# Split weight pieces on GpSimd's DMA queue, and fp8 tokens scaled by ScalarE

## The chip, the cores and the metric

The kernel runs on one core of a Trainium2 chip. The metric is the device time of one execution, in microseconds. The core has five engines that each follow their own list of instructions in order: TensorE (matrix products and transposes), VectorE, ScalarE, GpSimd, and SyncE (SP), which here only issues DMAs. ScalarE and GpSimd can issue DMAs too. In the profile they are called PE, DVE, ACT, POOL and SP; PEld is TensorE's loading of weights. Engines wait for each other through semaphores, and a waiting instruction holds up all that stands behind it on its engine.

## The reference

Two layers of a gated cross-attention block over x, 4 x 512 tokens of 512 features. The first adds an int8 cross-attention to the context and a mixture of experts; the second an fp8 attention with 16 query heads on 8 key heads, and a ternary feed-forward layer. Cut to what matters here:

```python
# layer 0, the experts: 8 experts, 2 per token, plus a shared one
order = jnp.argsort(flat_sel, stable=True)
routed_in = xf[order // TOPK] * top_scores_sorted[:, None]
h = silu(ragged_dot(routed_in, w1, counts)) * ragged_dot(routed_in, w3, counts)
routed_out = ragged_dot(h, w2, counts)

# layer 1, the fp8 attention
def _div_clamp_fp8(x, scale):
    y = jnp.clip(x / scale, -448., 448.)
    return fp8_roundtrip(y.astype(bfloat16))
ln_out = _ln(x, ln_w, ln_b)
q  = _ln(linear(_div_clamp_fp8(ln_out, q_in_scale), wq) * wq_scale, qln_w, qln_b)
k, v, qx  = (the same with scales of their own)
core, xout = softmax(q k / sqrt(128)) v, the same for qx with the context's keys
out = linear(_div_clamp_fp8(concat(core, xout), proj_smooth), wproj) * scales
```

So the tokens are normalized, given an affine, and then divided by four different input scales (q, qx, k, v), each followed by a clip, a rounding to bf16 and one to fp8. The scales are vectors over the features, not scalars.

## The kernel before, in words

The work runs in four stages on the time axis of the profile: the int8 cross-attention (to about 510 us); the routing and the shared expert (to about 703 us); the expert slots and after them the context's keys and values (to about 1360 us); and the fp8 attention with the ternary feed-forward woven in (to the end).

**Split weights.** The fp8 attention's matrix products run in a two-part format: a weight is kept as a high part and a remainder, both fp32r. `split_weights` (L1493 on) cuts the weights in 80 pieces of 128 x 512. A piece (class `Split`) has four steps: `load` brings 256 KB to the tile s_raw (L1519); `centre` multiplies by the input scale (L1525) and, for the query and key heads, takes out the mean over each head (`centred`, L1488 to L1490), on VectorE; `cut` lets ScalarE round to the high part (L1531) and GpSimd subtract it from the whole (L1532), both into s_hl; `store` writes 512 KB to DRAM (L1535). s_raw and s_hl have two buffers each. Of the pieces, 23 are done during the shared expert, step by step in a written order (those carry L245, the line of the helper that records an ordered instruction). The other 57, 33 with centring and 24 of the projection without, are done in the slots, through `__call__`.

**Slots.** Tokens sorted by expert fill 39 slots of 128 rows (loop at L1290). For each slot s, TensorE transposes the rows (`turn_in`), multiplies by w1 and w3 (`up`), transposes the hidden row (`turn_hidden`) and multiplies by w2 (`down`); ScalarE applies silu (L1243), VectorE the gate's product (L1244), and ScalarE scales the result (L1262) and stores it. The weights of an expert come in with `load` (L1193 to L1200, two DMAs of 896 KB) and `load_down` (L1222), on SP's queue, only where the expert differs from that of the slot two before; `load` of slot s + 3 overwrites the buffer of slot s + 1. Rows are loaded and stored on ScalarE's queue. Each pass of the loop also takes one or two split pieces and one step of the ternary weights (t_raw: loads at L2276, sums, scales and codes at L2283 to L2308, stores at L2309; all DMAs on SP). In this stage only TensorE's order is written by hand; a scheduler (Tile) orders the instructions of each other engine by its own estimate of when they can run, and the order that it chooses is fixed in the program.

**Attention.** 32 units (batch, head pair, source) of 16 ticks each. A `Beat` holds for each tick a list of steps by place; the places in order are begin, gate, weighed, divide, evacuate, normal, turned, squares, gated, scores, weigh, project, turn_in, turn, rest, codes, load. All engines are ordered by hand here, so the place fixes the position in each engine's list. The exponentials on ScalarE (g_p) are in "scores". `tokens` (L1930 on) prepares the next batch's tokens while the present one is attended to, for b = 1, 2, 3: load (g_xn), normalize, transpose on TensorE to PSUM (`turn`, place turn_in), `affine` on VectorE to g_ln (place normal), and 16 `code` steps (place codes). A code step calls `scaled` (L1629, VectorE: times the input scale, then the minimum with 448, to a bf16 tile f_y of two buffers) and `coded` (L1618, VectorE: the maximum with -448, the exponent mask f_e, the constant f_c; then two additions on GpSimd, f_t and the result g_xq). The attention's outputs and the feed-forward's rows go through `scaled` and `coded` too.

Evacuations of transposed probabilities (g_pT) go to VectorE or ScalarE, by how much else is entered for the tick; `affine` enters one step for VectorE in that count (the last argument of `at`).

Of the kernel before, what the change touches and what calls it, by code (L numbers as in the profile page):

```python
# [12 lines left out]
BF = mybir.dt.bfloat16  # L13
# [4 lines left out]
AF = mybir.ActivationFunctionType  # L18
ALU = mybir.AluOpType
# [3 lines left out]
P = 128  # L23
B, S, D = 4, 512, 512
# [3 lines left out]
KC = D // P  # L28
# [9 lines left out]
FP8_MAX = 448.0  # L38
# [136 lines left out]
class Router:  # L175
# [46 lines left out]
    def partial(self, PE, pg, b):  # L222

        for c in range(KC):
            PE.matmul(
                pg[ts(c, 32)], lhsT=self.gw[:, c, :], rhs=self.xT[b][:, c, :],
                start=True, stop=True,
            )
# [19 lines left out]
class Beat:  # L248
# [10 lines left out]
    def at(self, tick, place, step, busy=None):  # L259

        if busy is not None:
            self.loads[tick, busy] = self.loads.get((tick, busy), 0) + 1
        self.steps.setdefault(tick, {}).setdefault(self.PLACES.index(place), []).append(step)
# [1220 lines left out]
def centred(k, w, heads, VE):  # L1484

    wv = w.rearrange("p (h d) -> p h d", d=D1)
    m = k.small.tile([P, heads], F32, tag="s_mean")
    VE.tensor_reduce(m, wv, AX.X, ALU.add)  # L1488
    VE.tensor_scalar(m, m, -1.0 / D1, None, ALU.mult)
    VE.tensor_tensor(wv, wv, m[:, :, None].to_broadcast([P, heads, D1]), ALU.add)  # L1490


def split_weights(k):  # L1493

    nc, tc, a = k.nc, k.tc, k.a  # L1500
    s = {
        "q": tc.dram_tile([NP, P, KC, 2, 512], F32, name="s_q"),
        "qx": tc.dram_tile([NP, P, KC, 2, 512], F32, name="s_qx"),
        "kv": tc.dram_tile([NP, P, KC, 2, 512], F32, name="s_kv"),
        "kx": tc.dram_tile([B, NP, TB, P, 2, 2, D1], F32, name="s_kx"),
        "proj": tc.dram_tile([NP, 2, HP, P, 2, 512], F32, name="s_proj"),
    }

    class Split:

        def __init__(self, of, to, scales=(), c=0, heads=0):
            self.of, self.to, self.scales, self.c, self.heads = of, to, scales, c, heads

        def load(self, pool, SY):
            self.pool = pool
            self.raw = pool.tile([P, 512], F32, tag="s_raw", name="s_raw")
            SY.dma_start(self.raw, self.of)  # L1519

        def centre(self, VE):
            n = len(self.scales)
            for i, name in enumerate(self.scales):
                part = self.raw[:, ts(i, 512 // n)]
                VE.tensor_scalar(part, part, k.col(name)[:, self.c : self.c + 1], None, ALU.mult)  # L1525
            if self.heads:
                centred(k, self.raw[:, 0 : self.heads * D1], self.heads, VE)

        def cut(self, AE, GE):
            self.hl = hl = self.pool.tile([P, 2, 512], F32R, tag="s_hl", name="s_hl")  # L1530
            AE.copy(hl[:, 0, :], self.raw)  # L1531
            GE.tensor_tensor(hl[:, 1, :], self.raw, hl[:, 0, :].bitcast(F32), ALU.subtract)  # L1532

        def store(self, SY):
            SY.dma_start(self.to, self.hl.bitcast(F32))  # L1535

        def __call__(self, pool):
            self.load(pool, nc.sync)
            self.centre(nc.vector)
            self.cut(nc.scalar, nc.gpsimd)  # L1540
            self.store(nc.sync)

    steps = []
    for i in range(NP):
        for name in ("q", "qx"):
            steps += [
                Split(a[f"w_{name}"][i, :, c, :], s[name][i, :, c], (f"{name}_in",), c, HP)
                for c in range(KC)
            ]
        steps += [  # L1550
            Split(a["w_kv"][i, :, c, :], s["kv"][i, :, c], ("k_in", "v_in"), c, 2)
            for c in range(KC)
        ]
        steps += [
            Split(a["w_proj"][i, src, h], s["proj"][i, src, h])
            for src in range(2) for h in range(HP)
        ]
    return s, steps


def attend_and_feed(k, scratch, codes8, sources, ffn):
# [13 lines left out]
    nc, tc, a = k.nc, k.tc, k.a  # L1575
    VE, AE, GE, PE = (Ordered(tc, e) for e in (nc.vector, nc.scalar, nc.gpsimd, nc.tensor))
    UNIT = HP * TB
    with ExitStack() as ctx:
        p1 = ctx.enter_context(tc.tile_pool(name="g_1", bufs=1))
        p2 = ctx.enter_context(tc.tile_pool(name="g_2", bufs=2))  # L1580
# [10 lines left out]
        scale = 1.0 / math.sqrt(D1)  # L1591
        rin = codes8.rin
# [23 lines left out]
        at = beat.at  # L1616

        def coded(y, out, n=S):  # L1618

            VE.tensor_scalar(y, y, -FP8_MAX, None, ALU.max)  # L1620
            e = p2.tile([P, S], U16, tag="f_e", name="f_e")[:, 0:n]
            c = p2.tile([P, S], BF, tag="f_c", name="f_c")[:, 0:n]
            VE.tensor_scalar(e, y.bitcast(U16), 0x7F80, None, ALU.bitwise_and)
            VE.tensor_scalar(c, e.bitcast(BF), 2.0**-6, 1.5 * 2.0**20, ALU.max, ALU.mult)
            t = p2.tile([P, S], F32, tag="g_ct", name="f_t")[:, 0:n]
            GE.tensor_tensor(t, y, c, ALU.add)
            GE.tensor_tensor(out, t, c, ALU.subtract)

        def scaled(src, j, n=S):  # L1629
            y = p2.tile([P, S], BF, tag="f_y", name="f_y")[:, 0:n]  # L1630
            VE.tensor_scalar(y, src, rin[:, j : j + 1], FP8_MAX, ALU.mult, ALU.min)
            return y

        def load_w(of, got, key, parts):
# [293 lines left out]
        def tokens(u0, b):  # L1928


            xq, got = [None] * 4, {}

            def stats(src):
                st = sm4.tile([P, 6], F32, tag="ln_st")
                mv = sm4.tile([P, 2], F32, tag="g_mv")
                VE.bn_stats(st, src)
                VE.bn_aggr(mv, st)
                ve = sm4.tile([P, 1], F32, tag="g_ve")
                VE.tensor_scalar(ve, mv[:, 1:2], EPS, None, ALU.add)
                rstd = sm4.tile([P, 1], F32, tag="g_lnr")  # L1940
                GE.tensor_tensor(rstd, ve, k.neghalf[:, :1], ALU.pow)
                return mv, rstd

            def norm(t, part):
                xn = got["xn"][:, t, :]
                if part:
                    mv, rstd = got["st", t]
                    VE.tensor_scalar(xn, xn, mv[:, 0:1], rstd, ALU.subtract, ALU.mult)
                if part < 2:
                    got["st", t] = stats(xn)  # L1950

            def turn(c):
                got["pt"] = pt = ps_p.tile([P, S], F32, tag="ps_p", name="ps_p")
                for t in range(TB):
                    PE.transpose(pt[:, ts(t, P)], got["xn"][:, t, ts(c, P)], k.ident)

            def affine(c):
                got["ln"] = lnT = p1.tile([P, S], F32, tag="g_ln", name="g_ln")
                VE.tensor_scalar(
                    lnT, got["pt"], k.col("ln_w")[:, c : c + 1], k.col("ln_b")[:, c : c + 1],  # L1960
                    ALU.mult, ALU.add,
                )

            def code(c, i):
                if c == 0:
                    xq[i] = codes8.place(i, F32R, f"g_xq{i}_{b}")
                coded(scaled(got["ln"], i * KC + c), xq[i][:, c, :])

            def fetch():
                got["xn"] = xn = p1.tile([P, TB, D], F32, tag="g_xn", name=f"g_xn{b}")  # L1970
                nc.sync.dma_start(xn, ffn.mid[ts(b, TB)].rearrange("t p d -> p t d"))

            at(u0, "load", fetch)
            for t in range(TB):
                for part in range(3):
                    at(u0 + 3 * t + 2 + part, "codes", partial(norm, t, part))
            for c in range(KC):
                m = u0 + UNIT + 1 + 4 * c
                at(m, "turn_in", partial(turn, c))
                at(m + 1, "normal", partial(affine, c), VE)  # L1980
                for n, i in enumerate((0, 2, 3)):
                    at(m + 1 + n, "codes", partial(code, c, i))
                m = u0 + 2 * UNIT + 11 + c
                at(m, "turn_in", partial(turn, c))
                at(m + 1, "normal", partial(affine, c), VE)
                at(m + 1, "codes", partial(code, c, 1))
            return xq

# [208 lines left out]
        xq = sources  # L2197
        for n, (b, i, src) in enumerate(units):
# [4 lines left out]
            if n + 1 < len(units):  # L2203
                nb, ni, nsrc = units[n + 1]
                if nb != b:
                    xq = following
# [213 lines left out]
```

## Time and profile before

| | |
|---|---|
| median of 3 runs | 3403.62 us (3402.86 to 3405.48) |
| the profiled execution, its time | 3405.26 us |
| its span | 3403.6 us |
| mean clock granted to TensorE | 0.983 |
| slots, L1262 of slot 0 to the end | 731 to about 1148 us |
| distance of undisturbed slots | 10.32 us |
| token stretches, first to last affine | 1753.4 to 1871, 2248 to 2367, 2744 to 2862 us |

The profile has the time from the first to the last instruction as its span. A line of the groups reads: source line, engine, operation, output tile <- input tiles with their shapes, the count; busy time in us and the mean of one in ns; the engine's idle time just before them and what ended it. A line of the windows gives the busy time of PE, PEld, DVE, ACT and POOL with instruction counts, then the granted clock, the share of the time in which the 16 DMA engines were busy, and GB/s. A line of the timeline gives the start, the length, and in brackets the idle time before. A line of the waits reads: who waited, for whom; total us, times, longest. SPq is SP's queue of DMA issues.

### The profile page before, as it was taken

The page shows a single profiled execution, that of the slowest core. Times are in us where ns is not written, and L with a number is a line of the kernel's source. Part 1 is how long each engine was busy: PE and PEld are TensorE (multiplying, and loading weights), DVE is VectorE, ACT ScalarE, POOL GpSimd, SP SyncE. Part 2 cuts the span into 40 slices and gives each one's busy share as a digit, 9 for nine tenths or more (in the row PEclk, how much of TensorE's full clock was granted, in tenths as well). Part 3 has the DMA queues.
Part 4 walks back from the last instruction along what each step waited for, and adds up shares of the span by engine and source line. Part 5 has one row for each costly group of instructions (what it writes and reads, how often), then busy time and mean ns, then how long its engine had stood idle before and what let it go on. Part 6 is the DMA issues. An engine that isn't in the chain of part 4 may idle for free.

```text
span 3403.6 us, 47697 instructions
## 1 busy us (share of the span) xinstructions
PE 3223.4 (95%) x15488; PEld 2144.5 (63%) x15488; DVE 2145.9 (63%) x4551; ACT 1573.2 (46%) x4524; POOL 1377.1 (40%) x1568
## 2 busy tenths in 40 slices
PE   7998899899889999899999999999999999999997
PEld 4555554345445444577777777767777767777775
DVE  6788786532362355265587676687666786666557
ACT  4666671122222233455554555544545545555543
POOL 2001013422121256245466554566544576544443
PEclk9999999999899999899999999999999999999998
DMA  5534334855765544422231423323333322333210
GB/s 164 152 113 121 75 83 146 305 172 181 257 227 203 173 143 164 168 94 101 104 112 66 149 97 113 107 87 106 121 107 108 103 100 89 113 118 102 91 67 24
DMA packets 222008, 436.15 MB, mean 128 GB/s; under 512 B 23616, under 2 KB 82496, under 8 KB 220096
## 3 DMA queue, kind: packets, MB, share of 16 engines
q1 hardware_dynamic: 205408, 395.87, 35.3%
q10 hardware_dynamic: 11232, 20.45, 1.9%
q0 software_dynamic: 5120, 16.78, 1.6%
q8 instruction: 125, 2.05, 0.2%
q14 instruction: 123, 1.01, 0.1%
HBM read 387.33 MB, written 100.20 MB: 143 GB/s over the span
## 4 chain that ended last, share of the span: by engine, by line
PE 62%; DVE 9%; DMA 4%; POOL 3%; issue 2%; ACT 1%; SPq 1%; DVEq 0%; POOLq 0%; ACTq 0%
PE ps_w L245 11%; PE pss L245 10%; PE ps_p L245 10%; PE ps_o L245 9%; PE ps_t L245 8%; PE m_pk L245 5%; PE po L245 2%; PE pu L245 2%; PE pw L245 2%; DVE f_y L245 2%; DMA t_raw<-in_w_gu_dram 1%; DMA s_raw<-in_w_proj_dram 1%; DVE nm L245 1%; DVE t_work L245 1%; DVE g_hn L245 1%
## 5 line engine op out<-in xcount | busy, mean ns | idle before, releaser
L245 DVE TENSOR_REDUCE nm<-pss 128x1 f32<-128x512 f32 x768 | 523.9, 685 | 126.8 <-PE pss L245 121.6
L245 PEld LDWEIGHTS ps_w<-g_pT,g_v 128*128 128x128 f32 x2048 | 388.6, 191 | 299.2 <-issue 223.5
L245 ACT ACTIVATE g_p<-pss,nm 128x512 f32<-128x512 f32 x512 | 350.6, 685 | 478.5 <-DVE nm L245 437.4
L245 PE MATMUL ps_w<-g_pT,g_v 128*128 128x256 f32 x2048 | 530.1, 382 | 23.7 <-DVE f_y L245 13.6
L245 PE MATMUL pss<-g_kT,g_qT 128*128 128x512 f32 x1024 | 524.1, 594 | 0.9 <-ACT g_p L245 0.9
L245 POOL TENSOR_SCALAR g_p<-g_p,rs 128x512 f32<-128x512 f32 x512 | 366.8, 717 | 382.4 <-DVE rs L245 365.8
L245 PE MATMUL ps_t<-ident,g_p 128*128 128x128 f32 x2048 | 307.5, 273 | 0.0
L245 POOL TENSOR_TENSOR g_rstd<-ss,neghalf 128x4 f32<-128x4 f32 (+1 forms) x192 | 184.8, 963 | 298.9 <-ACT ss L245 298.7
L245 PE MATMUL ps_o<-g_wp,g_cq 128*128 128x512 f32 x1024 | 287.3, 423 | 0.0
L245 PE MATMUL ps_p<-g_wq,g_xq 128*128 128x512 f32 x1024 | 281.8, 417 | 5.5 <-DMA g_wq<-s_q 5.1
L245 DVE COPY g_pT<-ps_t 128x512 f32<-128x512 f32 x244 | 167.0, 684 | 166.2 <-PE ps_t L245 165.8
L245 POOL TENSOR_TENSOR f_t<-f_y,f_c 128x512 f32<-128x512 bf16 (+1 forms) x180 | 206.2, 1146 | 155.8 <-DVE f_c L245 86.9
L245 ACT COPY g_pT<-ps_t 128x512 f32<-128x512 f32 x268 | 155.9, 582 | 234.7 <-PE ps_t L245 234.7
L245 PEld LDWEIGHTS ps_t<-ident,g_p 128*128 128x128 f32 x2048 | 243.8, 141 | 26.3 <-POOL g_p L245 1.1
L245 ACT ACTIVATE p<-pss,nm 128x512 f32<-128x512 f32 x256 | 177.5, 693 | 143.1 <-DVE nm L245 139.8
L245 PE MATMUL m_pk<-m_wx,m_ctxT 128*128 128x512 f32 x512 | 230.0, 592 | 0.0
L245 PEld LDWEIGHTS ps_o<-g_wp,g_cq 128*128 128x128 f32 x1024 | 196.9, 192 | 41.6
L245 PEld LDWEIGHTS ps_p<-g_wq,g_xq 128*128 128x128 f32 x1024 | 191.1, 190 | 49.4 <-issue 6.0
L1532 POOL TENSOR_TENSOR s_hl<-s_raw,s_hl 128x512 fp32r<-128x512 f32 x57 | 76.5, 1352 | 342.4 <-ACT s_hl L1531 322.5
L245 DVE RECIPROCAL rs<-g_sm 128x1 f32<-128x1 f32 x512 | 82.6, 161 | 202.8 <-ACT g_p L245 200.9
L245 ACT ACTIVATE junk<-ps_p 128x128 f32<-128x128 f32 x640 | 176.7, 276 | 67.4 <-PE ps_p L245 53.2
L1244 DVE TENSOR_TENSOR m_work<-m_work,pw 128x448 f32<-128x448 f32 x39 | 24.2, 620 | 254.1 <-PE pw L245 217.7
(341 smaller groups left out, 5915.4 us busy)
## 6 DMA issues: line engine op xcount, KB each, us to landing
m_w<-in_w_dram SPq DMA_DIRECT2D x117, 896.0 KB
g_wp<-s_proj SPq DMA_DIRECT2D x128, 512.0 KB
g_wq<-s_q SPq DMA_DIRECT2D x128, 256.0 KB
g_wq<-s_qx SPq DMA_DIRECT2D x128, 256.0 KB
st_k<-hl_k SPq DMA_DIRECT2D x128, 128.0 KB
st_q<-hl_q SPq DMA_DIRECT2D x128, 128.0 KB
s_proj<-s_hl SPq DMA_DIRECT2D x32, 512.0 KB
s_kx<-m_ring SPq DMA_DIRECT2D x64, 256.0 KB
```

The costliest lines, as they stand in the source:

```text
L245: return lambda *args, **kw: self.tc.keep_in_program_order(call(*args, **kw))
L1244: nc.vector.tensor_tensor(work[:, 2, 0:HID], work[:, 2, 0:HID], pw, ALU.mult)
L1532: GE.tensor_tensor(hl[:, 1, :], self.raw, hl[:, 0, :].bitcast(F32), ALU.subtract)
```

## The change

For the 57 pieces in the slots, load and store are issued by GpSimd, not SP; the 23 pieces before them stay as they were. In the attention, `coded` now clips on both sides in one operation and `scaled` only multiplies. For the tokens, the affine goes from VectorE (place normal, entered in the count) to ScalarE (place turned, not entered), and the multiplication by the input scale from VectorE (place codes) to ScalarE (new function `scale_token`, place gated, in the same tick as its code step). The attention's outputs and the feed-forward's rows still multiply on VectorE.

```diff
         def __call__(self, pool):
-            self.load(pool, nc.sync)
+
+            self.load(pool, nc.gpsimd)
             self.centre(nc.vector)
             self.cut(nc.scalar, nc.gpsimd)
-            self.store(nc.sync)
+            self.store(nc.gpsimd)
...
         def coded(y, out, n=S):
 
-            VE.tensor_scalar(y, y, -FP8_MAX, None, ALU.max)
+            VE.tensor_scalar(y, y, FP8_MAX, -FP8_MAX, ALU.min, ALU.max)
...
         def scaled(src, j, n=S):
             y = p2.tile([P, S], BF, tag="f_y", name="f_y")[:, 0:n]
-            VE.tensor_scalar(y, src, rin[:, j : j + 1], FP8_MAX, ALU.mult, ALU.min)
+            VE.tensor_scalar(y, src, rin[:, j : j + 1], None, ALU.mult)
             return y
...
             def affine(c):
                 got["ln"] = lnT = p1.tile([P, S], F32, tag="g_ln", name="g_ln")
-                VE.tensor_scalar(
-                    lnT, got["pt"], k.col("ln_w")[:, c : c + 1], k.col("ln_b")[:, c : c + 1],
-                    ALU.mult, ALU.add,
+                AE.activation(
+                    lnT, got["pt"], AF.Identity, scale=k.col("ln_w")[:, c : c + 1],
+                    bias=k.col("ln_b")[:, c : c + 1],
                 )
+
+            def scale_token(c, i):
+                got["y"] = y = p2.tile([P, S], BF, tag="f_y", name="f_y")
+                j = i * KC + c
+                AE.activation(y, got["ln"], AF.Copy, scale=rin[:, j : j + 1])
 
             def code(c, i):
                 if c == 0:
                     xq[i] = codes8.place(i, F32R, f"g_xq{i}_{b}")
-                coded(scaled(got["ln"], i * KC + c), xq[i][:, c, :])
+                coded(got["y"], xq[i][:, c, :])
...
             for c in range(KC):
                 m = u0 + UNIT + 1 + 4 * c
                 at(m, "turn_in", partial(turn, c))
-                at(m + 1, "normal", partial(affine, c), VE)
+                at(m + 1, "turned", partial(affine, c))
                 for n, i in enumerate((0, 2, 3)):
+                    at(m + 1 + n, "gated", partial(scale_token, c, i))
                     at(m + 1 + n, "codes", partial(code, c, i))
                 m = u0 + 2 * UNIT + 11 + c
                 at(m, "turn_in", partial(turn, c))
-                at(m + 1, "normal", partial(affine, c), VE)
+                at(m + 1, "turned", partial(affine, c))
+                at(m + 1, "gated", partial(scale_token, c, 1))
                 at(m + 1, "codes", partial(code, c, 1))
```

## The prediction

> **What bounds the kernel now.** I read the engines' busy time first, then the busy time by stage, then the waits, and last the timeline of one place that the waits point to.
>
> ```profile
> PE 3223.4 (95%) x15488; PEld 2144.5 (63%) x15488; DVE 2145.9 (63%) x4551; ACT 1573.2 (46%) x4524; POOL 1377.1 (40%) x1568
> ```
>
> TensorE sets the time nearly everywhere, so an edit can gain only where TensorE stands idle, or lose by making it idle elsewhere. The change touches two stages: the 39 expert slots (703 to 1148 us), and three stretches of the attention in which the next batch's tokens are coded. Their busy times, in the columns TensorE, weight load, VectorE, ScalarE, GpSimd, clock, DMA share:
>
> ```profile
> 703.00:844.00 141.00, 139.17 (x428) 72.47 (x429) 38.18 (x79) 34.57 (x59) 25.28 (x20) 0.99 0.48 162
> 844.00:1018.00 174.00, 145.59 (x424) 73.76 (x423) 84.28 (x144) 39.44 (x67) 38.19 (x27) 0.92 0.69 237
> 1018.00:1142.00 124.00, 124.00 (x386) 64.48 (x385) 30.06 (x54) 27.20 (x47) 13.04 (x11) 1.00 0.54 188
> 1750.30:1779.80 29.50, 27.64 (x134) 20.22 (x133) 27.21 (x53) 15.51 (x51) 23.92 (x24) 1.00 0.32 109
> 1779.80:1813.30 33.50, 29.03 (x129) 21.10 (x128) 29.55 (x59) 12.10 (x32) 25.77 (x26) 0.95 0.27 85
> ```
>
> The slots run full at both ends and lose time in the middle. The slots' last scaling (L1262) comes every 10.32 us where nothing disturbs it; summed over all slots the spacing exceeds that by 38.7 us, all of it between 865 and 1018 us. Why, the waits and the timeline say:
>
> ```profile
> POOL s_hl L1532 <- ACT s_hl L1531: 322.5, 41, 14.8
> SPq L1535 <- POOL s_hl L1532: 222.8, 55, 10.5
> ```
>
> ```profile
> 865.12 1.57 SPq L1535 DMA_DIRECT2D s_qx<-s_hl  x2
> 866.78 0.41 SPq L1519 DMA_DIRECT2D s_raw<-in_w_qx_dram  x1
> 867.28 1.50 SPq L1519 DMA_DIRECT2D s_raw<-in_w_kv_dram  x1
> 870.54 1.12 SPq L1200 DMA_DIRECT2D m_w<-in_w_dram  x2
> ```
>
> SP's queue is in order. It stood from 854.5 to 865 in a piece's store (L1535) that waits for GpSimd's subtraction, so the next expert's weights (L1200), whose buffer was free at about 861, were asked for at 870.54, and TensorE waited 10.89 us for them, until 876.51.
>
> **Part 1: the pieces' loads and stores on GpSimd's queue.** It takes 57 loads (256 KB) and 57 stores (512 KB), 114 DMAs, off SP. That removes the blocking above. At most it returns the 38.7 us, since with the slots at 10.32 each nothing remains; taken alone it would end the slots at 1110.
>
> What it adds. Setting the two instruction orders side by side, GpSimd's queue now holds per piece: subtract k (L1532), store k, load k+2, in that order, since there are two buffers of each kind. And with SP free the scheduler hands out the pieces faster: up to three centres stand on VectorE between two slots' gates (L1244), all 57 are through by slot 20 of 39; before, they lasted to about slot 37. VectorE and ScalarE are in order, so a gate behind three pieces waits for these pieces, and TensorE for the gate. The first 20 slots thus end no earlier than the 57 pieces. Their own time is 20 x 10.32 = 206 us; what counts is whether 57 pieces need more.
>
> Before shows no plain DMA from GpSimd. The nearest row is its indirect DMA of the same 256 KB, and the same piece's cycle with SP's queue just ahead of the slots:
>
> ```profile
> 691.90 1.27 POOL L245 TENSOR_TENSOR s_hl<-s_raw,s_hl 128x512 fp32r<-128x512 f32 x1 [2.70 <-ACT s_hl L245]
> 695.88 1.27 POOL L245 TENSOR_TENSOR s_hl<-s_raw,s_hl 128x512 fp32r<-128x512 f32 x1 [2.71 <-ACT s_hl L245]
> ```
>
> ```profile
> 598.27 0.96 POOL L1135 DMA_INDIRECT slots_in<-m_rows,r_posi  x1 [0.30 <-issue]
> ```
>
> ```profile
> L1135 POOL DMA_INDIRECT slots_in<-m_rows,r_posi x32: 956/985/2253, 567.0 to 631.6; - x32
> L1532 POOL TENSOR_TENSOR s_hl<-s_raw,s_hl x57: 1254/1267/2028, 705.0 to 1118.7; 128x512 fp32r<-128x512 f32 x57
> ```
>
> Ahead of the slots a piece took 3.97 us, 7.95 for two buffers: subtraction 1.27, 1.3 to the load's issue, 3.01 from issue to use, and the rest centring and cast. On GpSimd one issue costs 0.985 plus the 0.30 gap, 1.29 us. From the load's start to its use I take 4.36: between 4.0 (0.985 + 3.01) and 4.71 (the gather at 1232.84, used at 1237.55). Centring is 2.2 us alone and 2.95 in company, say 2.58; the cast 0.69; a subtraction in the slots 1.35 on average. A centred piece's loop is 1.35 + 1.29 + 4.36 + 2.58 + 0.69 = 10.27 us for two, 5.13 each; 33 of them, 169 us. For the 24 pieces of the projection (no centring) the loop would give 3.85 each, but GpSimd itself needs 1.35 + 2 x 1.29 = 3.93; 94 us. The sum is 263 us. About 5 us more where the ternary coding (0.9 to 1.85 us an operation) falls among the pieces, in slots 14 to 18. Excess 263 + 5 - 206 = 62 us, against 38.7 now: **+23 us**. Slots 21 to 39 then run alone at 10.32. Bounds: if an issue costs only SP's 0.34 plus the gap, and a landing 3.0, centred pieces take 3.9 and the others 2.8, together 196 us, under the slots' own 206: -38.7. If every issue took the row's maximum, 2.25 + 0.3, GpSimd alone needs 6.45 a piece, 368 us: +128.
>
> Two rules of the Trainium skill speak against the change. "DMA: Bandwidth & Descriptors", section on issuing engines, says that issuing from several engines saves only the sequencer's time. The row above differs: SP held an expert's load behind a waiting store for 9.5 us. By the rule the 38.7 us would stay and part 1 could only cost; by the row the blocking goes, and I take the row. "SBUF — State Buffer", on the trap that VectorE sets for GpSimd's DMAs, says that the descriptors are written by GpSimd, which VectorE's fast modes lock out: 620 ns become 3100. The row holds 0.985 in the median with VectorE at work and 2.25 at worst, so some issues do meet it. By the row +23; with 3.1 + 0.3 for each issue, 8.15 a piece, it would be about +220. I take the row's median and keep the rule for a rival.
>
> **Part 2: tokens on ScalarE.** Per coded batch (three of them) 8 affines and 16 scalings leave VectorE:
>
> ```profile
> L245 DVE TENSOR_SCALAR f_y<-g_ln,r_in 128x512 bf16<-128x512 f32 x48 | 37.2, 776 | 0.0
> L245 DVE TENSOR_SCALAR g_ln<-ps_p,pcol_sb 128x512 f32<-128x512 f32 x24 | 19.2, 799 | 14.0 <-PE ps_p L245 14.0
> ```
>
> VectorE loses 56.4 us. ScalarE gains 24 x 0.77 (its row with scale and bias from PSUM, 774 ns) + 48 x about 0.70 (between its SBUF cast, 618, and that 774) = 52 us, and hands some five copies of g_pT the other way. TensorE was idle 1.86 + 4.47 = 6.3 us in the two windows, 7.7 us over a batch's whole stretch, 23 us for three: the most that can come. Half of it stays, I estimate: GpSimd is busy 23.9 of 29.5 and 25.8 of 33.5 us there, its additions for the codes take 2.4 us each, and the new scaling waits for one of only two f_y buffers, ahead of the exponentials on ScalarE. **-12 us**, bounds -23 and +3.
>
> The two clips in one operation: as many instructions as before, and the same shapes; f_c, which already has two operations on bf16, takes 314 ns. So 0, hidden or not; even 0.05 us on 180 of them would be 9 us of VectorE, covered outside the token stretches by its idle time.
>
> **Sum.** 3405.3 (the profiled execution) + 23 - 12 = 3416; the median of the runs lies 1.6 lower: 3415.
>
> **The rivals.** A, faster: GpSimd's plain DMA is cheaper than its indirect one. The issue then takes 0.34 to 0.7 us, the pieces 196 to 230 us, the slots come to -39 to -10, and with -12 the time is 3353 to 3382, say 3370. For it: an indirect DMA also reads a list of rows. Against: the descriptors are GpSimd's work in both. The point at which it decides: at 4.42 us a piece (252 us) excess and token gain cancel. B, much slower: issues starved behind VectorE, half of them at the maximum: 1.92 an issue, 5.77 and 5.19 us a piece, 315 us, +75; 3467. For it: the centres run on VectorE in just these microseconds. Against: the median of 985. C: the token half gives nothing, because GpSimd is the next bound and the scaling holds the exponentials up (+3): 3430.
>
> **How the numbers follow.** Likeliest as summed, 0.50; A 0.27; B 0.12; C 0.11. A measurement of this kernel tells 0.2%, 6.8 us, from no change. Of the likeliest, 3395 to 3435, 0.05 is faster, 0.15 same, 0.30 slower; of A 0.25 faster, 0.02 same; B slower; C 0.09 slower and 0.02 same. Sum: faster 0.30, same 0.19, slower 0.51. The range leaves out the lower half of A and most of B: 3370 to 3458.
>
> **What would show it.** Right: no wait of SP for L1532 in the slots; L1200 issued when its buffer is free; in slots 1 to 20 the spacing of L1262 at 12 to 14 us, then 10.32; GpSimd's DMAs near 1 us; all pieces done at 960 to 985 us. In the token stretches TensorE idle 3 to 5 us a batch instead of 7.7. Wrong: DMAs on GpSimd at 0.5 us and slots at 10.32 from the start (A); at 2 us (B); f_y named as what ScalarE waits for ahead of g_p (C); or slots that don't wait for their pieces at all.

## The result, and the profile after

The changed kernel takes 3414.74 us in the median of 11 runs (3408.93 to 3422.67), the kernel before 3406.18 in as many (3402.86 to 3411.56): ratio 1.0027, 95% interval 1.0019 to 1.0035. It is 8.6 us slower, and 3415 was forecast. But that is luck in good part: the sum came out right because two of its terms were wrong by similar amounts. The profiled execution of the changed kernel took 3419.88 us, 5 more than its median. The first line of the profile of the changed kernel:

```profile
PE 3226.1 (94%) x15469; PEld 2145.2 (63%) x15488; DVE 2100.2 (61%) x4485; ACT 1614.2 (47%) x4590; POOL 1433.4 (42%) x1682
```

The slots up to the first product of the context's keys, which starts at 1190.1 us (before: 1148.3). First the kernel before, then the changed one in two stretches: to the last of the pieces, and from there. Columns: length, busy time of PE, PEld, DVE, ACT, POOL, then clock, DMA share, GB/s.

```profile
703.00:1148.30 445.30, 415.06 (x1248) 213.43 (x1249) 152.53 (x275) 102.26 (x173) 76.51 (x57) 0.97 0.58 200
```

```profile
703.00:1000.00 297.00, 239.00 (x664) 120.19 (x665) 113.00 (x218) 66.58 (x118) 137.19 (x170) 0.89 0.69 232
1000.00:1190.10 190.10, 190.10 (x586) 98.25 (x586) 36.08 (x60) 33.27 (x55) 0.00 (x0) 1.00 0.38 122
```

The slots take 41.8 us longer. Of these, 27.8 are idle time of TensorE: 30.2 us before, 58.0 after, all of it in the first stretch. The other 14.0 are the same matmuls busy for longer, 429.1 us in all against 415.1; the granted clock was 0.93 on average (0.89 in the first stretch), against 0.97 before. The second stretch is full, as forecast for slots without pieces. What TensorE waited for in the slots, before and then after (total us, times, longest):

```profile
PE pu L245 <- DMA m_w<-in_w_dram: 19.7, 4, 10.9
PE po L245 <- DMA m_w<-in_w_dram: 8.7, 4, 2.8
```

```profile
PE pu L245 <- ACT m_work L112: 54.1, 14, 12.2
PE pu L245 <- ACT s_hl L1531: 4.9, 1, 4.9
```

The waits for an expert's weights are gone: 28.4 us to nothing. In their place TensorE waits for ScalarE's copy of the next rows (L112; 1.4 us before). The timeline of the changed kernel shows one such wait:

```profile
761.27 0.62 ACT L1531 CAST s_hl<-s_raw 128x512 fp32r<-128x512 f32 x1 [4.59 <-DMA s_raw<-in_w_proj_dram]
761.80 0.54 ACT L1243 ACTIVATE m_work<-pu 128x448 f32<-128x448 f32 x1
...
763.86 0.62 ACT L1531 CAST s_hl<-s_raw 128x512 fp32r<-128x512 f32 x1 [1.53 <-DMA s_raw<-in_w_proj_dram]
764.38 0.58 ACT L112 COPY m_work<-pt 128x512 f32<-128x512 f32 x1
...
765.02 1.86 PE L245 MATMUL pu<-m_w,m_work 128*128 128x448 f32 x2 [4.83 <-ACT m_work L112]
```

ScalarE stood 4.59 and then 1.53 us in casts of pieces that were still on their way; silu and copy stood behind them in order, and TensorE behind the copy. VectorE and ScalarE hold each other up in the same way. In the first stretch, after the change:

```profile
ACT s_hl L1531 <- DVE s_raw L1490: 116.2, 24, 13.4
ACT s_hl L1531 <- DMA s_raw<-in_w_proj_dram: 74.3, 23, 12.6
DVE m_work L1244 <- ACT m_work L1243: 77.0, 10, 16.8
```

The casts waited 116.2 us for VectorE's centring (49.3 before, up to 1000 us) and 74.3 for loads (7.1 before); VectorE's gate product, with the next centrings behind it, waited 77.0 us for the silu behind the casts. GpSimd's issues and the landing of its loads, from the same trace (the first two lines show the projection's 24 pieces, in ns; the landing is that of all loads on L1519):

```profile
L1519 POOL DMA_DIRECT2D s_raw<-in_w_proj_dram x24: 541/541/1063, 742.8 to 987.4; - x24
L1535 POOL DMA_DIRECT2D s_proj<-s_hl x24: 536/565/575, 750.2 to 995.0; - x24
DMA to landing us min/median/max: 2.8/4.7/11.9
```

The tokens run on ScalarE at 783 ns an affine and 722 ns a scaling, near the 770 and 700 that the sum used:

```profile
L245 ACT ACTIVATE f_y<-g_ln,r_in x48: 705/722/727, 1794.5 to 2877.7; 128x512 bf16<-128x512 f32 x48
L245 ACT ACTIVATE g_ln<-ps_p,pcol_sb x24: 767/783/784, 1793.7 to 2876.7; 128x512 f32<-128x512 f32 x24
```

From the first product of queries and keys to the last the attention took 1898.3 us before (1426.5 to 3324.8) and 1873.7 after (1467.0 to 3340.7).

### The profile page after: what moved, and what is told of

It is laid out like the page before. It is cut to its first block, busy times and chain, and to the rows that moved or that the text cites. A ratio compares the mean times of both kernels' runs of the same rounds, so it can differ in the third digit from the quotient of the medians.

```text
span 3418.2 us, 47621 instructions
## 1 busy us (share of the span) xinstructions
PE 3226.1 (94%) x15469; PEld 2145.2 (63%) x15488; DVE 2100.2 (61%) x4485; ACT 1614.2 (47%) x4590; POOL 1433.4 (42%) x1682
## 3 DMA queue, kind: packets, MB, share of 16 engines
q8 instruction: 125, 2.05, 0.2%
## 4 chain that ended last, share of the span: by engine, by line
PE 62%; DMA 6%; DVE 6%; POOL 4%; ACT 2%; issue 2%; SPq 0%; ACTq 0%; DVEq 0%; POOLq 0%
PE ps_w L245 11%; PE pss L245 11%; PE ps_p L245 10%; PE ps_o L245 9%; PE ps_t L245 8%; PE m_pk L245 5%; PE po L245 2%; DMA s_raw<-in_w_proj_dram 2%; PE pu L245 2%; PE pw L245 2%; POOL s_hl L1532 1%; DMA s_raw<-in_w_kv_dram 1%; DMA t_raw<-in_w_gu_dram 1%; DVE t_work L245 1%; DVE g_hn L245 1%
## 5 line engine op out<-in xcount | busy, mean ns | idle before, releaser
L245 PE MATMUL pu<-m_w,m_work 128*128 128x448 f32 x312 | 158.0, 590 | 59.0 <-ACT m_work L112 54.1
L245 PEld LDWEIGHTS pt<-ident,p 128*128 128x128 f32 x1024 | 119.1, 142 | 96.8 <-issue 47.5
```

Source lines behind the costliest of these rows:

```text
L245: return lambda *args, **kw: self.tc.keep_in_program_order(call(*args, **kw))
```

## The experiments

**The two halves apart.** First the pieces alone, from the kernel before:

```diff
         def __call__(self, pool):
-            self.load(pool, nc.sync)
+            self.load(pool, nc.gpsimd)
             self.centre(nc.vector)
             self.cut(nc.scalar, nc.gpsimd)
-            self.store(nc.sync)
+            self.store(nc.gpsimd)
```

> Only the pieces' loads and stores on GpSimd's queue; the attention as before. Theory: the changed kernel's slots end 42 us later (first product of the context's keys at 1190.1 against 1148.3) and its attention is 26 us shorter, and the two halves don't touch each other. So this one is 38 to 44 us slower than before, about 3447 us, with the first product of the context at 1190. Rival, the later start is made good in the attention whatever the tokens do (transfers that are further ahead): 3415 to 3425 us.

Measured: 3438.4 us against 3405.6 of before on the same chip, ratio 1.0098 (1.0081 to 1.0115), +32.8 us. That is less than the 38 to 44 expected, which were read from the changed kernel's profiled execution with its 5 us above the median. The first product of the context is at 1180.1. TensorE waits 50.4 us for L112.

The attention half alone is the rest of the change's diff, with both queues left at SP.

> Only the attention half (tokens scaled on ScalarE, the clips in one operation); the pieces on SP as before. Theory: 24 to 28 us faster than before, about 3380 us, with the slots unchanged (first product of the context at 1148). My forecast's term of -12 would give 3394. Rival, the attention is shorter in the changed kernel only because it starts later: 3400 to 3406 us.

Measured: 3381.8 us, ratio 0.9928 (0.9912 to 0.9945), -23.8 us, just under the 24 to 28 expected; the slots end as before (first product at 1149.8). Together 32.8 - 23.8 = +9.0, against 8.6 for both at once: the halves add up, so they hardly touch each other. The rival in both expectations, that the attention made good a late start, is out.

**Inside the attention half.** The clips alone:

```diff
         def coded(y, out, n=S):
-            VE.tensor_scalar(y, y, -FP8_MAX, None, ALU.max)
+            VE.tensor_scalar(y, y, FP8_MAX, -FP8_MAX, ALU.min, ALU.max)
...
-            VE.tensor_scalar(y, src, rin[:, j : j + 1], FP8_MAX, ALU.mult, ALU.min)
+            VE.tensor_scalar(y, src, rin[:, j : j + 1], None, ALU.mult)
```

> Only the two clips in one operation, on VectorE as before, no token on ScalarE. Theory: 0, within 3 us of before, since the number of operations and their shapes are the same. Rival, the clips carry a part of the 26 us, since an operation with one scalar operand less is shorter: 5 to 12 us faster, with a shorter mean of the operations that write f_y.

Measured: 3404.9 us, ratio 1.0001 (0.9991 to 1.0010). Its attention takes 1898.3 us, to the tenth what it took before. The clips are worth nothing that these runs can show.

The affine alone on ScalarE, the scaling still on VectorE, with the clips:

```diff
             def affine(c):
...
-                VE.tensor_scalar(
-                    lnT, got["pt"], k.col("ln_w")[:, c : c + 1], k.col("ln_b")[:, c : c + 1],
-                    ALU.mult, ALU.add,
+                AE.activation(
+                    lnT, got["pt"], AF.Identity, scale=k.col("ln_w")[:, c : c + 1],
+                    bias=k.col("ln_b")[:, c : c + 1],
                 )
...
-                at(m + 1, "normal", partial(affine, c), VE)
+                at(m + 1, "turned", partial(affine, c))
```

> Only a part of the attention half: the 24 affines on ScalarE (not entered in the count), the clips in one operation, but the 48 scalings still on VectorE; pieces on SP. The whole half brought 24 us, where my forecast had 12. Theory: VectorE's queue ahead of f_y is what TensorE waits for, so the gain goes with the time taken off VectorE (19.2 of 56.4 us): 6 to 10 us faster than before, 3396 to 3400 us. Rival, the place of the affine counts (TensorE and its next transpose wait for it, the count hands a copy to ScalarE): most of the 24 us, 3382 to 3388 us.

Measured: 3398.8 us, ratio 0.9982 (0.9974 to 0.9990), -6.0 us. The number is the expected one, the reason is not. The whole attention before, with the affine alone, and with the attention half:

```profile
1426.50:3324.80 1898.30, 1867.80 (x9629) 1416.87 (x9628) 1284.74 (x2805) 994.27 (x3021) 1017.40 (x1166) 1.00 0.31 102
```

```profile
1425.50:3318.40 1892.90, 1862.55 (x9630) 1414.99 (x9629) 1276.74 (x2787) 1007.24 (x3039) 1017.78 (x1166) 1.00 0.31 103
```

```profile
1428.40:3301.70 1873.30, 1857.54 (x9630) 1413.33 (x9629) 1244.69 (x2739) 1038.64 (x3087) 1014.54 (x1166) 1.00 0.31 104
```

With the affine alone TensorE stands idle for 30.4 us, as before (30.5); what shrinks, by 5.2 us, is the busy time of the same matmuls. So 19.2 of the 56.4 us that leave VectorE, a third, bring a quarter of the gain and none of the idle time. By difference the place of the affine isn't the main cause and the scalings bring the other 18 us; they were not moved alone. TensorE's longest waits, before and then with the attention half:

```profile
PE ps_w L245 <- DVE f_y L245: 11.8, 9, 1.9
PE ps_w L245 <- DVE rs L245: 8.5, 4, 2.7
```

```profile
PE ps_w L245 <- DVE rs L245: 4.3, 3, 1.4
PE ps_o L245 <- DVE t_work L245: 2.8, 6, 0.5
PE ps_w L245 <- DVE f_y L245: 2.7, 6, 0.6
```

The half's 25 us have two parts. TensorE's idle time falls from 30.5 to 15.8 us. And the same matmuls (9629 and 9630 records) are busy for 10.3 us less. That second part was not in the forecast, which counted idle time alone. The traces show where most of it comes from. In the attention before, the granted clock is 0.50 in four stretches of 3.4 us (from 1783.4, 2278.3, 2295.4 and 2790.3) and 1.00 elsewhere. Each begins within 0.6 us of the end of a wait of TensorE for VectorE that lasted 1.9 to 2.7 us. The last of the four, and four matmuls first at the full and then at the halved clock:

```profile
2790.30:2793.70 3.40, 3.30 (x8) 2.69 (x9) 2.60 (x6) 0.78 (x2) 3.09 (x4) 0.50 0.01 2
1789.24 1.03 PE L245 MATMUL ps_w<-g_pT,g_v 128*128 128x256 f32 x4
2790.40 2.05 PE L245 MATMUL ps_w<-g_pT,g_v 128*128 128x256 f32 x4 [2.72 <-DVE rs L245]
```

The four matmuls take twice as long at half of the clock, so the four stretches cost 6.8 us (an estimate, half of 4 x 3.4). With the affine alone there are two such stretches; with the whole half, whose longest wait is 1.4 us, there is none. The other 3.5 of the 10.3 us stay open.

**What costs in the slots: the order.** How many casts of these pieces stand on ScalarE between one slot's silu and the next, in the order in which the traces show them (the first number is ahead of slot 0; the 23 pieces before the slots are not counted):

```
before        2 0 1 1 1 1 2 2 2 0 2 2 2 2 2 2 2 2 2 2 2 2 2 2 2 2 2 1 1 1 1 1 1 1 1 1 1 1 0 0
pieces alone  2 2 3 3 3 4 2 2 3 3 4 3 3 3 2 1 3 2 2 4 3 0 0 0 0 0 0 0 0 0 0 0 0 0 0 0 0 0 0 0
held back     0 2 2 2 2 2 2 2 2 2 2 2 2 2 2 2 2 2 2 2 2 2 2 2 1 1 1 1 1 1 1 1 1 1 1 0 0 0 0 0
```

The next kernel holds the pieces back on VectorE and ScalarE by an order-only dependency, with the pieces on GpSimd's queue and the attention as before:

```diff
+        def after(self, engine, it):
+            first = getattr(self, "behind", {}).get(engine)
+            if first is not None:
+                tc.add_manual_dep(
+                    it.ins, first,
+                    mybir.DependencyInfo(
+                        mybir.DependencyClass.NoSync, mybir.DependencyReason.SCHED_ONLY
+                    ),
+                    reason="no sooner than the slot",
+                )
...
-            AE.copy(hl[:, 0, :], self.raw)
+            self.after("AE", AE.copy(hl[:, 0, :], self.raw))
...
-        def __call__(self, pool):
-            self.load(pool, nc.sync)
+        def __call__(self, pool, gate, silu):
+            self.load(pool, nc.gpsimd)
+            self.behind = {"VE": gate, "AE": silu}
...
-            nc.scalar.activation(work[:, 2, 0:HID], pu, AF.Silu)
-            nc.vector.tensor_tensor(work[:, 2, 0:HID], work[:, 2, 0:HID], pw, ALU.mult)
+            one = nc.scalar.activation(work[:, 2, 0:HID], pu, AF.Silu)
+            two = nc.vector.tensor_tensor(work[:, 2, 0:HID], work[:, 2, 0:HID], pw, ALU.mult)
+            got["behind", s] = two.ins.name, one.ins.name
...
-                split.pop(0)(ps)
+                split.pop(0)(ps, *got["behind", s])
```

> The pieces on GpSimd's queue, but held back in the order: a piece's first centring stands behind the gate, and its cast behind the silu, of the slot in whose pass it is handed out, so that one or two pieces stand between two silus up to slot 34, as before, and not two or three up to slot 20. The attention as before. Theory: the loss lies in the faster pace, which ties the slots to the pieces, and not in the queue; then SP's blocking is gone and the slots lose 0 to 15 us instead of 38.7: 3368 to 3383 us. Rival, the longer way through GpSimd's queue costs at any pace (landing 4.7 us from the issue in the changed kernel): as slow as with the pieces alone, 3430 to 3450 us.

Measured: 3404.5 us, ratio 0.9994 (0.9985 to 1.0003). The same queue and the same work as with the pieces alone, and 34 us less: the hurried order is what cost, and the rival, that the way through GpSimd's queue costs at any pace, is out. But the 38.7 us didn't come back either, so the expectation of 3368 to 3383 was wrong. In its slots TensorE waits for the same copy, less long:

```profile
PE pu L245 <- ACT m_work L112: 25.3, 9, 7.2
```

Its timeline shows what holds the copy, a cast whose load was issued at 896.89, ten microseconds before:

```profile
896.89 1.09 POOL L1531 DMA_DIRECT2D s_raw<-in_w_proj_dram  x2
...
907.77 1.27 ACT L1545 CAST s_hl<-s_raw 128x512 fp32r<-128x512 f32 x2 [6.62 <-DMA s_raw<-in_w_proj_dram]
...
908.95 0.58 ACT L112 COPY m_work<-pt 128x512 f32<-128x512 f32 x1
909.43 0.69 ACT L1263 ACTIVATE m_y<-po,tg 128x512 f32<-128x512 f32 x1
909.58 1.44 PE L245 MATMUL pu<-m_w,m_work 128*128 128x448 f32 x2 [3.95 <-ACT m_work L112]
```

**A later place, an even spread, or both.** In the first of three kernels a piece stands behind the copies of its pass (`got["behind"]` filled from them), in place of gate and silu. The cut diff is against the held-back kernel:

```diff
-            turn_hidden(s)
+            got["behind"] = [turn_hidden(s).ins.name, None]
             if s + 2 < SLOTS:
-                turn_in(s + 2)
+                got["behind"][1] = turn_in(s + 2).ins.name
...
-                split.pop(0)(ps, *got["behind", s])
+                split.pop(0)(ps, *got["behind"])
```

> As the held-back kernel (pieces on GpSimd's queue, attention as before), but a piece's cast stands behind ScalarE's copy of the next rows' transpose (L112) of the same pass, and its centring behind VectorE's copy of the hidden row (L110). In the held-back kernel TensorE no longer waited for an expert's weights (28 us before) but waited 25.3 us for that copy, which stood behind casts whose 256 KB came 10 us after their issue. Theory: what costs is a slot's operation that stands behind a piece's late load, not the number of pieces in a slot; then most of the 25 us goes, and the time is 3375 to 3390 us. Rival, the load on the DMA engines (85% busy from 880 to 940 us) sets the slots whatever the order: within 6 us of before, 3400 to 3411 us.

Measured: 3396.9 us, ratio 0.9977 (0.9969 to 0.9985): 8 us faster than before, between the two expectations. TensorE still waits 23.5 us for L112, in a profiled execution that took 3404.73 us, 8 more than the median.

The even spread replaces two pieces a pass and then one by 57 over 36 passes (NS is the number of pieces at the start of the loop), behind gate and silu as in the held-back kernel:

```diff
-            for _ in range(-(-len(split) // max(1, SLOTS - 5 - s))):
+            for _ in range((s + 1) * NS // 36 - s * NS // 36 if s < 36 else 0):
```

> The held-back kernel with the even spread alone: pieces on GpSimd's queue, 1.6 a slot over 36 passes, each behind the gate and the silu of its slot (not behind the later copies); the attention as before. With both, the time was 3370.9 us; with the later place alone 3396.9, held back without either 3404.5. If the spread does the work, 3372 to 3382 us; if both are needed, 3388 to 3400.

Measured: 3391.8 us, ratio 0.9963 (0.9950 to 0.9975): 13 us faster than before without the later place, within the second of its two expectations (both are needed).

Both together:

> The same, with the 57 pieces spread evenly over 36 passes (1.6 a slot) instead of two a slot and then one. Theory as above: equal to the kernel without the even spread or up to 8 us faster (3370 to 3388 us), since order decides and not number. Rival, number and transfers decide: clearly faster than it, by 10 us and more.

Measured: 3370.9 us, ratio 0.9900 (0.9884 to 0.9917), -34 us. The rival came true: 26 us below the later place alone, where up to 8 were expected. So my theory that order decides and not number was wrong as put: the later place alone gives 8, the spread alone 13, both 34. With both, the first product of the context is at 1112.0 us, where 1110 is what the slots need at 10.32 each, and only this wait is left in them:

```profile
PE pu L245 <- ACT m_work L112: 6.4, 5, 3.5
```

**Is the queue of any use?** The same order rules with both DMAs back on SP:

```diff
-            self.load(pool, nc.gpsimd)
+            self.load(pool, nc.sync)
...
-            self.store(nc.gpsimd)
+            self.store(nc.sync)
```

> The order of the fastest so far (evenly spread, behind the copies), but with the pieces' loads and stores on SP's queue as before; the attention as before. Theory: part of before's loss was SP's queue standing in a store while an expert's weights were due; that remains here, so 8 to 25 us slower than with GpSimd's queue: 3379 to 3396 us, with SP waiting in the stores for GpSimd and TensorE for expert weights. Rival, the queue doesn't matter and the spread of the pieces alone did it: 3366 to 3375 us.

Measured: 3408.2 us, ratio 1.0012 (1.0003 to 1.0020). SP's waits and TensorE's in its slots:

```profile
SPq L1549 <- POOL s_hl L1546: 227.5, 52, 10.9
```

```profile
PE pu L245 <- DMA m_w<-in_w_dram: 23.2, 8, 4.6
PE po L245 <- DMA m_w<-in_w_dram: 5.4, 2, 4.5
```

These are before's waits again (222.8 us of SP in the stores, 28.4 of TensorE for weights). Under the same rules for the order GpSimd's queue is worth 37 us, more than the 8 to 25 expected; on SP's queue the new order is worth nothing. The scheduler's orders differ a little: 0 to 3 casts between two silus here, the last behind the silu of slot 38, against 0 to 2 and slot 36 on GpSimd's queue. So the 37 us are those of the queue with the order that follows from it.

**Both kernels beaten.** The evenly spread, later pieces on GpSimd's queue with the attention half:

> Pieces on GpSimd's queue, evenly spread and behind the copies, and the attention half of the change (tokens on ScalarE). The two parts lie in different stages and have added up so far (33 - 24 = 9 against 8.6 measured), so 3370.9 - 24 = 3347 us, between 3343 and 3351. If they share something after all, 3355 or more.

Measured: 3348.6 us (3346.3 to 3353.6), ratio 0.9840 (0.9824 to 0.9857), 56 us faster than before and within the expectation.

## Why the prediction was right, and where it was not

- *SP's blocking costs, and the queue takes it away.* Right. 28.4 us of waits for weights vanish, and return when the DMAs go back to SP. By the rule of the Trainium skill that the forecast set aside ("DMA: Bandwidth & Descriptors", issuing engines are not separate DMA queues), further issuing engines save only the time to initiate a DMA; the waits would have stayed. What moved here was a wait in an in-order queue, not an issue.
- *The order ties the slots to their pieces.* Right: slots of 14.1 us on average up to slot 20, 10.32 from then on, no piece after 995 us (960 to 985 were forecast); holding the pieces back takes 34 us off. That ScalarE's copy would be the first to suffer was not said; the forecast named the gate.
- *The size, +23.* Too small: +32.8 measured. The step that failed is the piece loop. Two of its terms were off, on opposite sides. An issue was put at 1.29 us, by the indirect DMA's row; it is 0.54 to 0.57 with a gap that was 0.30 us or less for all but one. The landing was put at 4.36 and is 4.7 in the median, up to 11.9. With the measured medians the loop still gives about 257 us for the pieces (an estimate: 33 x 5.05 + 24 x 3.76), no more than the forecast's 263. But the subtractions run from 702.1 to 984.1 with the pieces alone, 282 us, and 288 in the changed kernel. The loop assumed that VectorE and ScalarE are free when a load lands; they stand behind each other's waits (116.2 and 77.0 us above), which no term held.
- *Tokens, -12 with a bound of -23.* Wrong in size: -23.8. The step that failed is the bound. It took TensorE's idle time in the three stretches as the most that can come, and the half of it as likely. As to idle time this was nearly right: 14.7 us came over the whole attention, and a batch's stretch has 3.0 us left, as forecast. The term at nothing was the busy time of the matmuls, 10.3 us, of which the granted clock explains some 6.8. GpSimd as the next bound (rival C) didn't show: TensorE's waits for f_y shrank from 11.8 to 2.7 us.
- *Clips, 0.* Right.
- *Rival A* had its premise (cheap issues) come true and its conclusion not: it put the pieces at 196 to 230 us. *Rival B*, issues starved behind VectorE: the longest of all 114 issues was 1.06 us, the typical load 0.54. The forecast had also taken the 620 and 3100 ns of "SBUF — State Buffer" for the length of an issue; the Trainium skill gives them there for a whole DMA.
- *Slips in the working.* The cast was put at 0.69 us; its row has 0.62. A batch's stretch had 7.3 to 7.6 us of idle TensorE, 22.3 in all, not 7.7 and 23. Neither changes the sum by more than some 2 us.

The total, 3415 against 3414.74, is therefore no proof of the working: +33 - 24 was forecast as +23 - 12.

## What to carry to other kernels

Moving DMAs to another queue also moves the scheduler's order on every engine that waits for them; set the two orders side by side, count what stands between two critical operations on each in-order engine, and hold the late work back if the count has grown. A relief that brings nothing may only be uncovering the next wait: here the queue alone gave +33, the queue with the later place and the even spread -34, and place and spread on the old queue nothing. And idle time of the bounding engine is not an upper bound of what its removal brings: look at its granted clock after each wait too.

## What the runs showed of the hardware

- A plain DMA issued by GpSimd costs it 0.54 us (load, 256 KB) to 0.57 us (store, 512 KB), about half of the indirect one of 256 KB (0.99 and 1.03 us in the medians of its two rows).
- The landing of 256 KB on GpSimd's queue took 2.8 to 11.9 us, the longest at 954.9, in a stretch (951 to 1000) in which the DMA engines were busy for 0.77 of the time.
- TensorE pays twice for some waits. In the attention before, four waits of 1.9 to 2.7 us each came with 3.4 us at a granted clock of 0.50, in which four matmuls took 2.05 us instead of 1.03. Not every such wait did: the one of 2.45 us that ended at 1800.91 did not. With the attention half the waits were 1.4 us at most, and the clock stayed at 1.00.
